# The last block of a four-block kernel: VectorE in the order written, Mamba steps spread singly

## The chip, the cores and the metric

The kernel runs on one core of a Trainium2 chip. The metric is the device time of one execution in microseconds (us). A core has five engines that run side by side and meet through semaphores: TensorE (PE; its weight loads are shown apart as PEld), VectorE (DVE), ScalarE (ACT), GpSimd (POOL) and SyncE (SP), which issues DMAs here. Each engine takes its own instructions in the order in which they stand in its queue.

## The reference

The input is `x`, 4 sequences of 1024 tokens with 128 channels. Four blocks follow each other, each of the form

```
xn = layernorm(x)
s  = attention-like layer(xn)
g  = silu(ffn-like layer(xn))
x  = x + s * g
```

Blocks 0 to 2 have softmax attention for `s` (16 heads of 8) and a channel mix or experts for `g`. The change is in block 3. There `s` is a Mamba-2 layer:

```
h       = layernorm(xn) * ln_w + ln_b
z, xBC, dt = split(h @ in_proj)
dt      = softplus(dt + dt_bias)
xBC     = silu(causal convolution of 4 taps over time (xBC))
state_t = state_(t-1) * exp(dt_t * A) + (dt_t * x_t) B_t;   y_t = state_t C_t + D * x_t
y       = y * silu(z);  y = y * rsqrt(mean(y^2) + eps) * rms_w
s       = xn + y @ out_proj
```

with 4 heads of 64 and 64 states. `g` is silu of a two-layer transformer on `xn` with 8 heads of 64, a local attention (windows of 64 tokens that look at themselves and the window before), and a gated GELU feed-forward of width 341. The two layers do not depend on each other until `s * g`.

## The kernel before

The kernel is written in a framework with tiles. The program is traced in the order in which Python emits instructions ("the order written"); then a planner orders each engine's instructions by its own estimate of when they can run. An instruction that is given to `keep_in_program_order` keeps its place on its engine. In the whole kernel all matmuls and transposes are kept so. For VectorE there is a wrapper, class `_Kept` (line 49): while its flag `on` is set, each VectorE instruction emitted through it is kept in the order written as well. The attention loops of blocks 0 to 2 set the flag (lines 561 to 591); before block 3 the plain `nc` is put back (`k.nc = nc`), so the planner orders VectorE there. ScalarE and GpSimd are ordered by the planner throughout.

Block 3 (`_block3`) weaves three lists of steps together; a step is a Python closure that emits some instructions:

- `local` (843 steps, the first 11 of them a lead-in): the two-layer transformer, 2 x 4 x 8 = 64 tiles of 128 tokens. In each turn of the loop over tiles, in this order: `scores` of tile i (TensorE into `lsc`, then VectorE's maxima `top` and `nb`), `turn` of i-1 (transposes `pt_ps`, copies `pT` on VectorE and ScalarE), `query` of i+2 (`qk_ps`; VectorE's rotation `qn`, `rot`; ScalarE's squares `sq`), `turn_out` of i-2, `key` of i+2, `weights` of i (8 exponentials `pr` on ScalarE), `to_fm` of i+1 (`qkt_ps`), `mix` of i-1 (`lo_ps`, then `rec` and `on`), `norms` of i+2 (VectorE's `ss`, GpSimd's power `rn`, line 1573, and scalings `qn`, `r8`), `out` of i-2 and `values` of i+2. Up to three places a tile, called `beside`, take a step from a side list: the shift of the next sequence, and for every four tiles the feed-forward `glu` as `[norm, None, normed, None, to_fm, gates, hidden, close]`, in the second layer followed by two steps that finish the output (`xn` on GpSimd, then the add into `x_end` on VectorE) with a `None` between. A `None` takes a place and emits nothing.
- `slots` from `_mamba` (206 slots, each a list of steps): the Mamba layer in 8 halves of 512 tokens. `put(at, step)` places a half's steps in slots around `at = 3 + 25 * h`: layer norm, transposes, projections of three channel groups (`project`, TensorE `xp_ps`, ScalarE into `cb`), the raw time steps, softplus, convolutions (`conv`, four VectorE instructions each into `xc`), running sums, gates (`z_ps`, then silu of `z` and `xc` on ScalarE), and then four chunks of 128 tokens, each with six steps from `exponents` (`xt_ps`, `r_ps`, `dec`) over `weights`, `products` (`y_ps`) and `turn` (`yt_ps`) to `norm` and `out` (`mo_ps`).
- `late`: what is left of block 2 (57 steps), at the block's start.

A layer norm has two halves: `_layernorm_parts` (line 80) computes mean and variance on VectorE (`ln_st`, `ln_mv`, `ln_ve`) and the factor `ln_rs` by a power on GpSimd (line 91), and returns a closure, called `normed` by its users, that scales the data on VectorE (line 95, four instructions). The small tiles of it have two buffers. All PSUM tiles of block 3 share a ring of eight buffers, so a matmul waits until the tile eight allocations back has been read.

`_interleave` emits from its lists in proportion to their lengths: first `local[:11]` with the first 9 slots, then the rest of `local` with the other 197 slots, where each slot's steps are emitted together. What is left of the feed-forward at the end (9 steps) follows.

Of the kernel before, what the change touches and what calls it, by code (L numbers as in the profile page):

```python
# [25 lines left out]
ALU = mybir.AluOpType  # L26
# [161 lines left out]
def _run(steps):  # L188
    for step in steps:
        if step:  # L190
            step()
# [960 lines left out]
def _mamba(k, t, wp, pool):  # L1152
# [6 lines left out]
    nc = k.nc  # L1159
    s = k.s  # L1160
    NH, HP, NS = 4, 64, 64
    ZX, HT = 644, 512
# [13 lines left out]
    conv_w = w3[:, ZX : ZX + 12].rearrange("p (g j) -> p g j", j=4)  # L1176
    conv_b = w3[:, ZX + 12 : ZX + 15]
# [10 lines left out]
    carry = wp.tile([P, 3, 3], F32, name="carry3")  # L1188
    dim = [P, 4, NH]

    def half_steps(h):
        v = Ctx()
        hf, n0 = h % 2, 4 * h
# [20 lines left out]
            matmul(xp, lhsT=w_in[:, c0 : c0 + P], rhs=v.xm, start=True, stop=True)  # L1214
            nc.scalar.copy(cb[:, 3 : HT + 3], xp)

        def conv(gq):
            if gq == 2:
                v.xc = pool.tile([P, 3, HT], F32, name="xc", bufs=1)
            cb = v.cb.pop(gq)  # L1220
            if hf == 0:
                nc.gpsimd.tensor_copy(carry[:, gq, :], cb[:, HT : HT + 3])
            acc = v.xc[:, gq, :]
            nc.vector.tensor_scalar(acc, cb[:, 0:HT], conv_w[:, gq, 0:1], conv_b[:, gq : gq + 1], ALU.mult, ALU.add)
            for j in range(1, 4):
                nc.vector.scalar_tensor_tensor(
                    acc, cb[:, j : j + HT], conv_w[:, gq, j : j + 1], acc, ALU.mult, ALU.add
                )
# [10 lines left out]
        def softplus():  # L1239


            raw, e = v.raw, v.e
            z, z2 = (pool.tile(dim, F32, name=f"dt_{i}", bufs=1) for i in "za")
            nc.vector.tensor_scalar_add(z, e, 2.0)
            nc.vector.reciprocal(z, z)
            nc.vector.tensor_tensor(z, z, e, ALU.mult)
            nc.vector.tensor_tensor(z2, z, z, ALU.mult)
            nc.vector.tensor_scalar_mul(e, z2, 2.0 / 17)
            for d in (15, 13, 11, 9, 7, 5, 3):
                nc.vector.scalar_tensor_tensor(e, e, 2.0 / d, z2, ALU.add, ALU.mult)  # L1250
            nc.vector.scalar_tensor_tensor(e, e, 2.0, z, ALU.add, ALU.mult)
            v.dt = pool.tile(dim, F32, name="dt", bufs=2)
            nc.vector.scalar_tensor_tensor(v.dt, raw, 0.0, e, ALU.max, ALU.add)
            v.da = pool.tile(dim, F32, name="da", bufs=2)
            nc.vector.tensor_tensor(v.da, v.dt, ea.unsqueeze(1).to_broadcast(dim), ALU.mult)
# [38 lines left out]

        v.cb = {}
        v.norm, v.to_fm, v.project, v.conv, v.raw_dt = norm, to_fm, project, conv, raw_dt
        v.softplus, v.sums, v.gates, v.weigh = softplus, sums, gates, weigh
        return v

    def chunk_steps(v, h, c, before):  # L1300
# [100 lines left out]
    slots = {}  # L1401

    def put(at, *steps):
        slots.setdefault(at, []).extend(steps)

    before = None
    for h in range(2 * B):
        v = half_steps(h)
        at = 3 + 25 * h
        put(at - 3, v.norm)  # L1410
        put(at - 2, lambda v=v: v.normed())
        put(at - 1, v.to_fm)
        put(at, v.raw_dt, lambda v=v: v.project(2))
        put(at + 1, v.softplus)
        put(at + 2, lambda v=v: v.conv(2), lambda v=v: v.project(0))
        put(at + 3, lambda v=v: v.conv(0), lambda v=v: v.project(1))
        put(at + 4, v.sums)
        put(at + 5, lambda v=v: v.conv(1))
        put(at + 6, v.gates)
        put(at + 7, v.weigh)  # L1420
        for c in range(4):
            u = before = chunk_steps(v, h, c, before)
            first = at + 8 + 4 * c
            for i, step in ((0, u.exponents), (1, u.weights), (3, u.products), (5, u.turn), (6, u.norm), (7, u.out)):
                put(first + i, step)
# [507 lines left out]
def _block3(k, t, out):  # L1933

    nc = k.nc
    s, xn = k.s, k.xn
    outv = out.rearrange("b (n p) c -> p (b n) c", p=P)
    with k.tc.tile_pool(name="w4", bufs=1) as wp, k.tc.tile_pool(name="l3", bufs=1) as pool, k.tc.tile_pool(
        name="ps3", bufs=1, space=PSUM
    ) as k.ps:  # L1940
        NW = 512 + 2 * HID + 384 + 8
        r4 = wp.tile([P, 2, 256], F32, name="r4")
        nc.sync.dma_start(r4.rearrange("p l c -> p (l c)"), t["r4"].to_broadcast([P, 512]))
        w4 = wp.tile([P, 2, NW], F32, name="w4")
        wqkv1 = wp.tile([P, 1536], F32, name="wqkv1")
        ends = {}

        def fetch(n):
            ends[n] = pool.tile([P, 4, C], F32, name="x_end", bufs=1)
            nc.sync.dma_start(ends[n], k.parked[n // 2][:, 4 * (n % 2) : 4 * (n % 2) + 4, :])  # L1950

        def finish(n, part):
            a = slice(4 * n, 4 * n + 4)
            if part == 0:
                nc.scalar.activation(xn[:, a, :], xn[:, a, :], AF.Silu)
                k.dump(3, n, s[:, a, :], xn[:, a, :])
                nc.gpsimd.tensor_tensor(xn[:, a, :], s[:, a, :], xn[:, a, :], ALU.mult)
            else:
                x = ends.pop(n)
                nc.vector.tensor_tensor(x, x, xn[:, a, :], ALU.add)  # L1960
                nc.sync.dma_start(outv[:, a, :], x)


        NW2 = 14 * P
        nc.sync.dma_start(w4[:, 1, 0:1024], t["w2"][:, 6 * P : NW2])
        nc.sync.dma_start(w4[:, 1, 1024:1030], t["w2"][:, NW2 + 6 : NW2 + 12])
        nc.sync.dma_start(w4[:, 1, 1030:1158], t["r2"][:, 2 * P : 3 * P].to_broadcast([P, P]))
        first, late = _late_steps(k, pool, w4[:, 1])
        _run(first)
        slots = _mamba(k, t, wp, pool)  # L1970
        local, begin, last = _local_layers(k, pool, w4, (k.wqkv0, wqkv1), r4, t["xpos"], xn, fetch, finish)
        _local_consts(k, pool)
        nc.sync.dma_start(w4[:, 0], t["w4"][:, 0, 1536:])
        late.append(lambda: nc.sync.dma_start(w4[:, 1], t["w4"][:, 1, 1536:]))
        nc.sync.dma_start(wqkv1, t["w4"][:, 1, 0:1536])

        def run(slot):
            for step in slot:
                step()


        slots = [lambda slot=slot: run(slot) for slot in slots]
        early = len(late) // 3
        _interleave(local[:begin], slots[:9], late[:early])

        n = 8 * (len(local) - begin) // (2 * NTILE + 2)
        m = n * (len(slots) - 9) // (len(local) - begin)
        _interleave(local[begin : begin + n], slots[9 : 9 + m], late[early:])
        _interleave(local[begin + n :], slots[9 + m :])
        run(last)  # L1990
# [3 lines left out]
def tile_blocks(ctx: ExitStack, tc: tile.TileContext, t, out, dump=None):  # L1994
    nc = tc.nc
    k = Ctx()
# [56 lines left out]
    k.parked = [tc.dram_tile([P, NT, C], F32, name=f"x{b}") for b in range(B)]  # L2053
    k.nc = _Kept(nc, tc)
    _blocks012(k, t)
    k.nc = nc
    stream.close()
    with tc.tile_pool(name="early3", bufs=1, side="right") as wp:
        _weights3(k, t, wp)
# [131 lines left out]
```

## Time and profile before

| | |
|---|---|
| time, median of 3 runs | 3529.68 us (3518.91 to 3532.71) |
| profiled execution, time | 3530.33 us |
| profiled execution, span from first to last instruction | 3528.6 us |
| granted TensorE clock, mean of the span | 0.960 |
| TensorE busy | 3137.5 us, 89% |
| VectorE busy | 2458.7 us, 70% |
| ScalarE busy | 1985.6 us, 56% |
| GpSimd busy | 1415.6 us, 40% |
| last block (2430 to 3530 us): TensorE, VectorE, ScalarE, GpSimd busy | 986.6, 829.3, 673.5, 691.0 of 1100 us |
| last block: granted clock | 0.93 |

A group row of the profile gives line, engine, operation, out<-in, shapes and count, then busy time and mean duration in ns, then the engine's idle time just before and what ended it. "A <- B: t, n, m" in a table of waits says that A stood idle for B, t us in n waits, the longest m. The granted clock is the share of TensorE's full clock that was given in a stretch. TensorE's ends are modelled, so its busy time is a reading of how densely it was fed.

### The profile page before, as it was taken

The numbers are of one execution on the slowest core, as the hardware profiler recorded it, in microseconds if no ns is written. First come the engines' busy times: TensorE is split into PE (matmuls) and PEld (weight loads), VectorE is DVE, ScalarE is ACT, GpSimd is POOL, SyncE is SP. The second block draws the span as 40 slices with busy tenths as digits, with TensorE's granted clock in tenths as the row PEclk, the third lists the DMA queues.
The fourth block names the chain that finished last, engine by engine and source line by source line (L and its number), as shares of the span: only waits on it lengthen the run. The fifth ranks groups of instructions, "written<-read, shape, count | busy, mean of one in ns | idle before, by whom it ended". The sixth has DMA issues, their size and how long they took to land.

```text
span 3528.6 us, 63440 instructions
## 1 busy us (share of the span) xinstructions
PE 3137.5 (89%) x23982; PEld 1693.8 (48%) x24121; DVE 2458.7 (70%) x4929; ACT 1985.6 (56%) x4191; POOL 1415.6 (40%) x1969
## 2 busy tenths in 40 slices
PE   4898988999989988889998989986899989989997
PEld 3444445664434434422333323322666767766665
DVE  7667663447777865788785686844788778777675
ACT  2444453346555554455666766664665656666664
POOL 5555553003323251120340321014766656755653
PEclk8999999999999999999999999998899999999999
DMA  3322312201222211011111211102110011011010
GB/s 101 71 63 55 73 42 87 59 28 47 52 50 60 42 51 31 21 45 28 39 45 45 66 35 26 30 7 73 29 37 16 20 25 24 18 24 28 21 27 21
DMA packets 134085, 146.61 MB, mean 42 GB/s; under 512 B 80642, under 2 KB 108298, under 8 KB 126474
## 3 DMA queue, kind: packets, MB, share of 16 engines
q1 hardware_dynamic: 131732, 138.34, 16.3%
q0 software_dynamic: 2048, 4.20, 0.4%
q8 instruction: 191, 3.13, 0.4%
q14 instruction: 114, 0.93, 0.1%
HBM read 94.42 MB, written 30.11 MB: 35 GB/s over the span
## 4 chain that ended last, share of the span: by engine, by line
PE 58%; DVE 19%; ACT 9%; POOL 8%; issue 4%; DMA 2%; SPq 0%; ACTq 0%; POOLq 0%; DVEq 0%
PE o_ps L104 11%; PE max_ps L104 10%; PE sc L104 10%; DVE neg L60 6%; ACT pt L451 4%; PE op L104 4%; PE hp L104 3%; POOL rn L1573 2%; PE proj_ps L104 2%; PE lsc L1481 1%; PE lo_ps L1481 1%; PE ag_ps L1481 1%; PE qk_ps L1481 1%; PE wo_ps L1481 1%; DVE xn L60 1%
## 5 line engine op out<-in xcount | busy, mean ns | idle before, releaser
L451 ACT ACTIVATE pt<-sc 128x512 f32<-128x512 f32 (+3 forms) x2432 | 1076.2, 512 | 754.1 <-PE sc L104 698.1
L60 DVE TENSOR_REDUCE neg<-max_ps 128x1 f32<-128x1024 f32 (+6 forms) x1088 | 1171.9, 1101 | 443.6 <-PE max_ps L104 404.8
L104 PE MATMUL sc<-q,k 128*128 128x512 bf16 (+3 forms) x2399 | 643.1, 340 | 94.6 <-ACT pt L451 69.0
L104 PE MATMUL max_ps<-k,q 128*128 128x512 bf16 (+3 forms) x2200 | 611.2, 347 | 73.8 <-DVE neg L60 50.7
L104 PE MATMUL o_ps<-pt,va 128*32 128x512 f32 (+3 forms) x4864 | 562.6, 526 | 16.8 <-POOL pt L421 9.1
L421 POOL TENSOR_SCALAR_AFFINE_SELECT pt<-pt 128x256 f32<-128x256 f32 (+2 forms) x768 | 291.3, 397 | 541.7 <-ACT pt L451 537.0
L104 PEld LDWEIGHTS <-k 128*128 128x128 bf16 x2432 | 185.6, 98 | 531.5 <-issue 415.9
L104 PEld LDWEIGHTS <-q 128*128 128x128 bf16 x2304 | 217.1, 99 | 357.6 <-issue 245.6
L1643 ACT ACTIVATE pr<-lsc,nb,r 128x128 f32<-128x128 f32 x512 | 201.2, 476 | 67.9 <-DVE nb L1635 67.7
L1564 POOL TENSOR_TENSOR qn<-qn,rot 128x512 f32<-128x512 f32 x128 | 166.1, 1303 | 157.8 <-DVE rot L1556 133.2
L1573 POOL TENSOR_TENSOR rn<-ss,neghalf 128x16 f32<-128x16 f32 x64 | 188.5, 2945 | 60.5 <-DVE ss L1571 48.3
L104 PEld LDWEIGHTS o_ps<-pt,va 128*32 128x32 f32 x4864 | 100.1, 109 | 227.1 <-issue 170.8
L196 POOL CAST negp<-neg 128x32 bf16<-128x32 f32 x48 | 10.1, 211 | 477.2 <-DVE neg L60 477.1
L91 POOL TENSOR_TENSOR ln_rs<-ln_ve,neghalf 128x4 f32<-128x4 f32 x72 | 73.8, 1026 | 262.0 <-DVE ln_ve L60 246.5
L728 ACT ACTIVATE h<-hp,eb 128x512 f32<-128x512 f32 x128 | 80.8, 683 | 163.2 <-PE hp L104 157.2
L1481 PE MATMUL qk_ps<-wqkv,hT 128*128 128x512 f32 x256 | 139.2, 628 | 23.7 <-DMA wqkv<-in_w_dram 7.3
L104 PE MATMUL hp<-xT,ew 128*128 128x512 f32 x256 | 127.9, 624 | 15.5 <-DVE neg L60 12.5
L60 DVE SCALAR_TENSOR_TENSOR xn<-op,gates,xn 128x128 f32<-128x128 f32 x256 | 72.0, 344 | 99.2 <-PE op L104 99.2
L104 PEld LDWEIGHTS op<-ew,h 128*128 128x128 f32 x1024 | 124.3, 194 | 19.6 <-issue 16.3
L104 PE MATMUL max_ps<-mask_window,ident 128*128 128x268 bf16 (+1 forms) x432 | 127.0, 294 | 0.0
L104 PE MATMUL op<-ew,h 128*128 128x128 f32 x1024 | 126.2, 277 | 0.1
L104 PEld LDWEIGHTS <-ident 128*128 128x128 bf16 x864 | 85.2, 99 | 65.5 <-issue 24.6
(368 smaller groups left out, 5483.9 us busy)
## 6 DMA issues: line engine op xcount, KB each, us to landing
q<-qx SPq DMA_DIRECT2D x144, 192.0 KB
k<-kx SPq DMA_DIRECT2D x432, 64.0 KB
va<-vb SPq DMA_DIRECT2D x120, 128.0 KB
qx<-qp SPq DMA_DIRECT2D x12, 768.0 KB
kx<-kp SPq DMA_DIRECT2D x12, 768.0 KB
ew<-in_e1w_dram SPq DMA_DIRECT2D x64, 128.0 KB
x<-x SPq DMA_DIRECT2D x16, 512.0 KB
x<-in_x_dram SPq DMA_DIRECT2D x8, 512.0 KB
```

The source lines that it names most:

```text
L60: r = op(*args, **kw)
L91: nc.gpsimd.tensor_tensor(rs, ve, k.neghalf[:, :n], ALU.pow)
L104: k.tc.keep_in_program_order(k.nc.tensor.matmul(*args, **kw))
L196: eng.tensor_copy(dst[:, 0], src)
L421: nc.gpsimd.affine_select(out=pt, in_=pt, pattern=[[0, 2], [step, pt.shape[2]]], compare_op=ALU.is_ge, fill=0.0, base=base, channel_multip ...
L451: nc.scalar.activation(pt[:, j % 2, :width], sc[:, :width], AF.Exp, scale=scale)
L728: nc.scalar.activation(h[:, hh, :], hp[:, hh, :], AF.Gelu, bias=eb1[:, e, hh : hh + 1])
L1481: pin(nc.tensor.matmul(*args, **kw))
L1564: nc.gpsimd.tensor_tensor(qn[:, i], qn[:, i], rot, ALU.add)
L1573: nc.gpsimd.tensor_tensor(rn, ss.rearrange("p w h -> p (w h)"), k.neghalf[:, : 2 * NH], ALU.pow)
L1643: nc.scalar.activation(t.pr[:, h, :], t.sc[r][:, c, :], AF.Exp, bias=t.nb[r][:, c : c + 1], scale=t.r8[:, h : h + 1])
```

## The change

Four things change, all in block 3:

1. The wrapper stays in use (`k.nc = nc` goes), and `_block3` sets its flag before it weaves the lists, so VectorE's instructions stand in the order written. (They then carry the wrapper's line, L60, in a profile.)
2. From slot 9 on, the Mamba slots are no longer emitted as units: their steps are put in one list, one entry each, an empty slot giving one empty entry (329 entries in place of 197 slots).
3. A convolution is split into two steps of two instructions each, with the next group's projection between the two for groups 2 and 0; the softplus is split into two steps (`softplus`, `series`), both in the same slot.
4. The Mamba layer norm's first half moves from slot `at - 3` to `at - 7`, its second half from `at - 2` to `at - 5` (not below slots 0 and 1).

```diff
-        def conv(gq):
-            if gq == 2:
+        def conv(gq, part):
+            if gq == 2 and part == 0:
                 v.xc = pool.tile([P, 3, HT], F32, name="xc", bufs=1)
-            cb = v.cb.pop(gq)
-            if hf == 0:
-                nc.gpsimd.tensor_copy(carry[:, gq, :], cb[:, HT : HT + 3])
+            cb = v.cb[gq] if part == 0 else v.cb.pop(gq)
             acc = v.xc[:, gq, :]
-            nc.vector.tensor_scalar(acc, cb[:, 0:HT], conv_w[:, gq, 0:1], conv_b[:, gq : gq + 1], ALU.mult, ALU.add)
-            for j in range(1, 4):
+            if part == 0:
+                if hf == 0:
+                    nc.gpsimd.tensor_copy(carry[:, gq, :], cb[:, HT : HT + 3])
+                nc.vector.tensor_scalar(
+                    acc, cb[:, 0:HT], conv_w[:, gq, 0:1], conv_b[:, gq : gq + 1], ALU.mult, ALU.add
+                )
+            for j in (1,) if part == 0 else (2, 3):
                 nc.vector.scalar_tensor_tensor(
                     acc, cb[:, j : j + HT], conv_w[:, gq, j : j + 1], acc, ALU.mult, ALU.add
                 )
...
             nc.vector.tensor_scalar_mul(e, z2, 2.0 / 17)
+            v.z, v.z2 = z, z2
+
+        def series():
+            raw, e, z, z2 = v.raw, v.e, v.z, v.z2
             for d in (15, 13, 11, 9, 7, 5, 3):
...
         at = 3 + 25 * h
-        put(at - 3, v.norm)
-        put(at - 2, lambda v=v: v.normed())
+        put(max(at - 7, 0), v.norm)
+        put(max(at - 5, 1), lambda v=v: v.normed())
         put(at - 1, v.to_fm)
         put(at, v.raw_dt, lambda v=v: v.project(2))
-        put(at + 1, v.softplus)
-        put(at + 2, lambda v=v: v.conv(2), lambda v=v: v.project(0))
-        put(at + 3, lambda v=v: v.conv(0), lambda v=v: v.project(1))
+        put(at + 1, v.softplus, v.series)
+        put(at + 2, lambda v=v: v.conv(2, 0), lambda v=v: v.project(0), lambda v=v: v.conv(2, 1))
+        put(at + 3, lambda v=v: v.conv(0, 0), lambda v=v: v.project(1), lambda v=v: v.conv(0, 1))
         put(at + 4, v.sums)
-        put(at + 5, lambda v=v: v.conv(1))
+        put(at + 5, lambda v=v: v.conv(1, 0), lambda v=v: v.conv(1, 1))
...
-        slots = [lambda slot=slot: run(slot) for slot in slots]
+        slots = [lambda slot=slot: run(slot) for slot in slots[:9]] + [
+            step for slot in slots[9:] for step in slot or [None]
+        ]
+        k.nc.on = True
         early = len(late) // 3
...
     _blocks012(k, t)
-    k.nc = nc
     stream.close()
```

More of the change, by code (lines that the diff above doesn't have):

```diff
@@ L1296, in half_steps @@
         v.norm, v.to_fm, v.project, v.conv, v.raw_dt = norm, to_fm, project, conv, raw_dt
-        v.softplus, v.sums, v.gates, v.weigh = softplus, sums, gates, weigh
+        v.softplus, v.series, v.sums, v.gates, v.weigh = softplus, series, sums, gates, weigh
         return v
```

## The prediction

> **What bounds the kernel now.** The change touches only the last block, so I first read the table of stretches for it: its start, its steady part (the 64 attention tiles) and its tail. The columns are the stretch, its length, the busy time and instruction count of each engine, the granted TensorE clock, the DMA share and GB/s.
>
> ```profile
> 2430.00:2530.00 100.00, 68.18 (x565) 45.67 (x566) 72.82 (x207) 49.23 (x95) 76.82 (x94) 0.80 0.20 57
> 2530.00:3477.00 947.00, 884.79 (x9566) 637.49 (x9568) 736.57 (x2074) 607.08 (x1285) 607.89 (x602) 0.94 0.11 24
> 3477.00:3530.00 53.00, 33.59 (x280) 22.87 (x278) 19.90 (x59) 17.18 (x29) 6.28 (x8) 0.86 0.05 16
> ```
>
> TensorE bounds it: in 947 us it is idle for 62.2 us only, and the next engine, VectorE (DVE), is busy for 737. But the clock is 0.94, so up to 0.06 x 947 = 57 us more of full-speed work is lost. What makes TensorE idle? It waits for VectorE, and VectorE waits for GpSimd (POOL). The waits of VectorE in the last block (who waits for whom, us in total, times, longest):
>
> ```profile
> DVE top L1632 <- PE lsc L1481: 39.2, 26, 2.9
> DVE sh L95 <- POOL ln_rs L91: 38.6, 13, 7.8
> DVE x_end L1960 <- POOL xn L1957: 19.2, 5, 5.3
> ...
> DVE ln_x L95 <- POOL ln_rs L91: 14.0, 3, 5.8
> DVE ss L1385 <- ACT sq L1382: 14.0, 9, 4.4
> ```
>
> The first row is harmless: VectorE has caught up with TensorE. The next three are a norm's second half, or the closing add, standing on VectorE before GpSimd has its factor. One such place in the chain that ended last (start, us, what):
>
> ```profile
> 2765.68 1.16 DVE ss L1571
> ...
> 2766.91 2.94 POOL rn L1573
> ...
> 2769.91 1.04 POOL qn L1574
> ...
> 2771.36 1.05 POOL ln_rs L91
> ...
> 2772.43 1.11 DVE sh L95 x4
> 2773.54 1.20 DVE top L1632 x2
> ...
> 2774.81 0.61 DVE pT L1653
> ...
> 2775.47 2.17 PE qkt_ps L1484 x8
> ```
>
> The norm's factor `ln_rs` queues on GpSimd behind `rn` (2.94), `qn` (1.04) and `r`: 5.3 us with its own 1.05. VectorE has `sh` next and sits idle for 3.95 us, though `top`, behind it, had its scores at 2767.7 (the matmuls end at 2766.45 + 1.21). So `top`, the exponentials and `pT` are late, TensorE finds no free PSUM buffer and stops for 3.05 us. What that costs shows in the stretches before, in, and after the stop:
>
> ```profile
> 2755.00:2771.00 16.00, 16.00 (x206) 12.31 (x195) 12.17 (x35) 10.36 (x22) 11.03 (x11) 1.00 0.18 35
> 2771.00:2775.00 4.00, 1.41 (x6) 0.58 (x6) 2.57 (x8) 0.10 (x1) 1.27 (x2) 0.95 0.01 2
> 2775.00:2785.00 10.00, 9.53 (x62) 8.22 (x63) 7.34 (x22) 6.58 (x17) 6.21 (x7) 0.51 0.01 2
> ```
>
> For 10 us after the stop the clock is halved: two `qk_ps` matmuls take 2.07 us in such a place and 1.02 elsewhere. Ten stops of this kind stand in the steady part of the timeline (VectorE's wait, then TensorE's idle time): 3.95 and 3.05 at 2772; 4.65, 3.82; 4.76, 3.44; 4.08, 2.52; 3.95, 3.38; 2.69, 1.83; 5.77, 3.90; 3.85, 1.58; 4.39, 3.40; 5.25, 3.86 at 3391. TensorE's sum is 30.8 us, half of its idle 62.2.
>
> **VectorE in the order written.** It adds and removes no instruction (4931 on VectorE both ways). Before, the planner of the framework put `sh` directly behind its sums. As written, an empty step stands between a norm's sums and its second half, about half a tile to one tile (8 to 16 us) later, and one between the two parts of the closing; in the order the new program has on VectorE, both scores of the next tile, `pT` and two projections stand between. That exceeds the 5.3 us GpSimd needs, so nine stops go (the tenth, `ss` behind `sq`, gets about 7 us from turn to norm and goes too). Idle time saved: 30.8 us.
>
> *The clock.* The Trainium skill, page "TensorE: Matmul & The Clock Gate", section "HAM oscillation", says that only idle gaps over about 3.4 us cost the clock. By it four of the ten stops pay (3.82, 3.44, 3.90, 3.86). The trace has half clock after eight of the ten, from 1.58 us (plus another 1.2 close by) and 3.05 us up, for 68.2 us, with TensorE busy 9.3 + 12.0 + 6.5 + 3.4 + 6.8 + 6.4 + 5.3 + 9.8 = 59.4 us. At full clock that work takes half: 29.7 us saved, by the rule's four stops (35.0 busy) 17.5. The measured eight decide; I take 25, since short matmuls follow the clock less.
>
> *The start.* `cl_ps` waits 10.39 us for `da`, as the 15 small instructions of the softplus (0.16 to 0.19 us each) were laid between convolutions and rotations from 2458.5 to 2469.8. As written they follow each other: 15 x 0.17 = 2.6, at the row's mean of 0.256 3.8 us. Saved: about 7.5; taken 8 with a little clock.
>
> *What else could it cost?* In a fixed order anything not ready blocks all behind it. By the times of before, most producers are done when TensorE passes the instruction's place in the new order. Exceptions: `wdt` (last of ScalarE's row after the gates; 8 places, at most 2.3 us late) and `dt_z` (8, at most 4.1). Behind them stand rotations and `ss`; TensorE has the ring of eight PSUM buffers before it notices. Bounds 0 and 8 x 6.4 = 51 us; the ten stops show that about 0.8 us of a wait is absorbed and most of these places have slack, so I take 5.
>
> **Slots step by step.** 197 slots become 329 single steps over the same 832 attention steps: one per 2.5 attention steps instead of a slot (one to four steps) per 4.2, so at 13.2 attention steps per 15.9 us tile 3.0 us against 5.1. All engines' work stays. The Mamba chain's distances on TensorE change; I laid the new TensorE order on the times of before:
> - products to turn (32): median 10.2 us before, 6.4 after, smallest 2.3. The chain between (`y`, `yi` on VectorE, `y` twice on GpSimd) ends 4.0 to 10.8 us after the first product, median 6.1; the products themselves give 2.3 more. At the median the shortfalls sum to 4.4 us, at 7.5 us to 16. Taken 5.
> - gates to first exponents (8): 10.7 before, 4.0 after. The last `xc` leaves ScalarE at -4.0 to +4.2 us from the gates' start, TensorE needs it at 4.1 to 8.1. Bounds 0 and 8 x 3; taken 4.
> - exponents to products in a half's first chunk (8): 5.3 to 17 us, needing 6.9 minus 1.2; taken 2, at the longest chain (12.8) 19.
> Their sum, 11, and the 5 above are 16 us lost, with ends 0 and about 110.
>
> **Convolutions in two steps.** Four instructions of 0.64 + 3 x 0.80 = 3.0 us become 1.4 and 1.6. It issues no more. The `cb` ring has two buffers: `project(1)` must await the second part of `conv(2)`, now one step (3 us) ahead; GpSimd's copy and ScalarE's eviction stand behind. Such waits for `xc` cost GpSimd 12.5 us in 840 now, idle time off the path. Taken 0, bounds -5 and +10.
>
> **Norm four slots sooner.** Eight sums (0.27, 0.165), an add, four scalings (about 0.5) on VectorE and one power (1.04) on GpSimd per half, no DMA. The sums and the second half now stand two to three steps, 6 us or more, apart. TensorE's own waits for `ln_x` (2.0 us in all) go: -2. It passes only the previous half's last chunks on VectorE and GpSimd; its 5 us are hidden by VectorE's 20% of idle time.
>
> **Sum.** -30.8 - 25 - 8 - 2 + 16 = -50 us. The profiled execution took 3530.3 us (span 3528.6), so 3480; the median of runs is 3529.7, which leaves 3480.
> A second way: six tiles, from 2615.2 to 2703.4, ran without a stop at clock 1.00 in 88.2 us, 14.7 each; all 63 tile periods average 15.9. If all ran at 14.7, 75 us would go. The sum stays inside this.
>
> **Rivals.**
> 1. *Quiet pace everywhere*: the stops with other causes go too. 75 + 8 from 3530 gives 3447. For it: VectorE was 80% busy in the quiet stretch (70.3 of 88.2). Against: seven stops of the steady part have table loads or `qn` as last releaser.
> 2. *Hidden*: the Mamba chain's shorter distances and VectorE's head waits return what the stops gave: 16 becomes 60, giving about 3525. For it: 48 places have less distance. Against: in the median they still fit.
> 3. *Slower*: GpSimd's `y` becomes the wait at turn. GpSimd holds `rn` for 2.94 us a tile; if half of the 32 turns wait 3 us and each brings 6.8 us of half clock (0.44 lost per us), 16 x 6.0 = 96 us come back: 3530 - 66 + 96 = 3560. It decides from 66 / 32 = 2.1 us per turn. Against: the median turn has 8.7 us for 6.1.
> 4. *The change does nothing*: excluded, as the built order on VectorE differs throughout the block.
>
> **How the numbers follow.** Chances: my sum 0.60 (its own range 3450 to 3510), rival 1 0.17, rival 2 0.12, rival 3 0.11. A measurement of this kernel can tell about 0.5%, 17.6 us: faster 0.77, same 0.12, slower 0.11. The range 3430 to 3535 reaches to rival 1 below, with some of what lies beyond the quiet pace, and takes in rival 2.
>
> **What would show it.** Right: VectorE's waits for `ln_rs` and for `xn` at the closing nearly vanish, the clock of the steady part rises from 0.94 to 0.97 or more, its TensorE idle time falls from 62 to below 45, and `cl_ps` waits 3 us. Wrong: TensorE's or its weight loads' waits at `yt_ps`, `xt_ps` or `y_ps` sum to over 40 us, or VectorE waits for `wdt`, `dt_z` or `ss` instead, at the same clock.

## The result, and the profile after

The changed kernel takes 3546.56 us (median of 11 runs, 3537.41 to 3552.26), the kernel before 3532.14 us in the runs beside it: a ratio of 1.0042, 95% interval 1.0032 to 1.0052. It is 0.4% slower; 1.4% faster was predicted (3480 from 3529.7), and 3546.56 lies outside the range of 3430 to 3535. The profiled execution took 3545.3 us with a span of 3543.3.

The table of stretches of the changed kernel (length, then TensorE, weight loads, VectorE, ScalarE, GpSimd busy, clock, DMA share, GB/s):

```profile
2430.00:2530.00 100.00, 71.07 (x568) 45.22 (x565) 76.22 (x207) 42.21 (x87) 76.11 (x95) 0.80 0.19 54
2530.00:3477.00 947.00, 868.14 (x9454) 617.26 (x9456) 786.44 (x2046) 605.81 (x1272) 599.23 (x591) 0.96 0.10 24
3477.00:3545.00 68.00, 48.26 (x394) 34.99 (x383) 29.02 (x82) 23.94 (x47) 16.19 (x19) 0.82 0.07 22
```

In the same 947 us the granted clock rose from 0.94 to 0.96, as the prediction wanted, but TensorE is idle for 78.9 us instead of 62.2, and got through 112 matmuls fewer. VectorE is busy 50 us longer (786.4 against 736.6), with no instruction more.

VectorE's waits in the last block of the changed kernel:

```profile
DVE top L60 <- PE lsc L1488: 33.3, 23, 6.4
DVE s L60 <- POOL rs L1394: 29.3, 14, 4.4
...
DVE ln_x L60 <- POOL ln_rs L91: 8.6, 1, 8.6
```

The row `sh <- ln_rs` (38.6 us in 13 waits) has shrunk to one wait of 1.1 us. A new row stands there: `s`, the last step of a Mamba chunk, waits 29.3 us for its factor `rs` from GpSimd. TensorE's waits from 2530 us on:

```profile
PE yt_ps L1170 <- POOL y L1378: 15.8, 8, 4.8
PE y_ps L1167 <- POOL xdt L1342: 9.8, 5, 3.0
PE qkt_ps L1491 <- POOL qn L1581: 8.0, 7, 3.6
PE ag_ps L1488 <- DVE gT L60: 6.3, 4, 4.0
```

Before, the largest were these, and neither of the two Mamba rows was among the first:

```profile
PE qkt_ps L1484 <- DVE pT L1653: 10.7, 4, 3.9
PE ag_ps L1481 <- DVE gT L1720: 6.0, 2, 5.1
```

Now the three largest are waits for GpSimd. One such place in the chain that ended last (start, us, what):

```profile
2970.57 1.27 POOL qn L1571
2971.84 0.53 POOL rs L1394
2972.39 0.35 DVE s L60
...
2972.87 0.42 DVE on L60
...
2973.84 1.20 DVE ss L60 x2
...
2975.32 2.91 POOL rn L1580
...
2978.30 1.04 POOL qn L1581
...
2979.73 0.73 POOL y L1367
...
2980.53 0.73 POOL y L1378
```

and its end on TensorE's timeline (start, us, what, idle time before it and who ended that):

```profile
2975.47 1.02 PE L1488 MATMUL qk_ps<-wqkv,hT 128*128 128x512 f32 x2
2981.31 0.69 PE L1170 MATMUL yt_ps<-ident,y 128*128 128x128 f32 x2 [4.82 <-POOL y L1378]
```

`rs` stands on GpSimd behind a rotation's addition. VectorE has `s` next and stops for 1.84 us; behind it, in the written order, stand `rec`, `on` and then `ss`, the norm of a later tile. So `ss` ends late, and GpSimd, which has `rn` next, is idle for 2.96 us. VectorE's own parts of `y`, whose products TensorE finished at 2971.6, come after `ss`, at 2975.3 to 2976.1. GpSimd's parts then stand behind `rn`, `qn` and `r` and begin at 2979.7, and the turn on TensorE waits for them. So a wait of 1.84 us at the head of VectorE's queue has gone through GpSimd's queue into another layer's chain. It can account for 1.84 of TensorE's 4.82 us at most. The rest comes from the order itself: VectorE's parts of `y` stand behind `ss`, and so GpSimd's parts stand behind `rn`, `qn` and `r`, which take 4.2 us.

### The profile page after: what moved, and what is told of

The parts are those of the page before. It is cut to its first block, busy times and chain, and to the rows that moved or that the text cites. A ratio compares the mean times of both kernels' runs of the same rounds, so it can differ in the third digit from the quotient of the medians.

```text
span 3543.3 us, 63508 instructions
## 1 busy us (share of the span) xinstructions
PE 3138.7 (89%) x23984; PEld 1686.5 (48%) x24121; DVE 2523.1 (71%) x4929; ACT 1985.1 (56%) x4188; POOL 1418.3 (40%) x1969
## 4 chain that ended last, share of the span: by engine, by line
PE 54%; DVE 21%; POOL 10%; ACT 8%; issue 4%; DMA 2%; SPq 0%; POOLq 0%; ACTq 0%; DVEq 0%
PE o_ps L104 11%; PE max_ps L104 10%; PE sc L104 9%; DVE neg L60 6%; ACT pt L451 4%; PE op L104 4%; PE hp L104 3%; POOL rn L1580 2%; PE ag_ps L1488 2%; PE proj_ps L104 2%; DVE xc L60 2%; DVE xn L60 1%; DVE ss L60 1%; PE lo_ps L1488 1%; PE lsc L1488 1%
## 5 line engine op out<-in xcount | busy, mean ns | idle before, releaser
L60 DVE TENSOR_REDUCE neg<-max_ps 128x1 f32<-128x1024 f32 (+6 forms) x1088 | 1172.8, 1103 | 442.8 <-PE max_ps L104 413.4
L104 PE MATMUL o_ps<-pt,va 128*32 128x512 f32 (+3 forms) x4864 | 560.8, 524 | 16.9 <-POOL pt L421 9.1
L60 DVE SCALAR_TENSOR_TENSOR xn<-op,gates,xn 128x128 f32<-128x128 f32 x256 | 72.1, 345 | 99.2 <-PE op L104 98.8
```

The costliest lines, as they stand in the source:

```text
L60: r = op(*args, **kw)
L104: k.tc.keep_in_program_order(k.nc.tensor.matmul(*args, **kw))
```

## The experiments

Every ratio is to the kernel before, from runs on the same chip, with its 95% interval. The table collects what I read from each trace: tiles (of 64) whose transposes on TensorE begin less than 0.4 us after GpSimd's last scaling of `qn`; turns (of 32) that begin less than 0.4 us after `y`; products (of 32) likewise after `dec` and `xdt`; and the time at half clock from 2530 us on, in the one profiled execution. A short link has next to no slack, and TensorE often stood waiting there: in the changed kernel it waited over 0.15 us 7 times for `qn` and 8 times for `y`. One execution says little of the clock (e3's profiled one, at 0.961, is below the median of e3's runs), so the column "clock" gives the mean granted clock in the median of all of a kernel's runs, and in brackets that of the kernel before beside it.

| kernel | VectorE | slots | short: `qn` | short: turn | short: products | half clock, us | clock | ratio |
|---|---|---|---|---|---|---|---|---|
| before | planner | whole | 2 | 0 | 0 | 119 | 0.960 to 0.962 | 1 |
| changed | written | single | 17 | 11 | 8 | 91 | 0.965 | 1.0042 |
| e1_order_alone | written | whole | 13 | 1 | 0 | 55 | 0.967 (0.962) | 0.9977 |
| e2_steps_alone | planner | single | 4 | 2 | 7 | 106 | 0.964 (0.962) | 0.9996 |
| e3_slots_whole | written | whole | 12 | 2 | 0 | 103 | 0.965 (0.962) | 0.9956 |
| e5_planner_order | planner | single | 4 | 5 | 4 | 98 | 0.964 (0.962) | 1.0017 |
| e6_norms_first | written | single | 7 | 13 | 7 | 82 | 0.968 (0.962) | 1.0049 |
| e7_turn_later | written | single | 20 | 0 | 7 | 99 | 0.964 (0.962) | 1.0010 |
| e8_whole_norms_first | written | whole | 6 | 2 | 0 | 62 | 0.967 (0.962) | 0.9944 |
| e9_half_power | written | single | 6 | 12 | 7 | 61 | 0.969 (0.962) | 0.9978 |
| e10_room | written | single | 19 | 0 | 5 | 115 | 0.962 (0.960) | 1.0093 |
| e11_before_half_power | planner | whole | 2 | 0 | 0 | 58 | 0.968 (0.960) | 0.9876 |
| e12_gates_later | written | whole | 8 | 2 | 0 | 47 | 0.970 (0.960) | 0.9915 |
| e13_norms_turn | written | single | 3 | 0 | 10 | 56 | 0.970 (0.961) | 0.9986 |
| e14_room_norms | written | single | 11 | 0 | 6 | 86 | 0.966 (0.961) | 1.0049 |
| e15_split_power | written | whole | 7 | 2 | 0 | 52 | 0.969 (0.961) | 0.9941 |

### The parts one by one

**e1_order_alone**: the kernel before, with VectorE's order fixed and nothing else.

```diff
+        k.nc.on = True
...
-    k.nc = nc
```

> The kernel before with VectorE kept in the order written in the last block, nothing else changed. Theory A (the written order takes the ten stops away as predicted, and the shorter Mamba distances of the single steps give it back, GpSimd's part of the chain being late at turn and products): this keeps the old distances, so it is faster than before by 30 to 60 us (ratio 0.983 to 0.992), with TensorE's waits at yt_ps and y_ps no longer than before (about 15 us together). Theory B (the fixed order on VectorE is itself the loss, since what is not ready blocks what stands behind): about +15 us or more, ratio 1.003 to 1.010, with VectorE waiting for GpSimd's rs or for ScalarE.

3519.42 us against 3526.26: 0.9977 (0.9965 to 0.9989). The order helps, by 7 us, where the prediction's terms for it (30.8 + 25 + 8 less 5) come to 59. Its profiled execution (3512.1 us, one of its faster ones) shows what it saves and what takes its place. VectorE's waits for `ln_rs` ahead of `sh` are down to one of 1.1 us, and half clock falls from 119 to 55 us; by the runs' clock, 0.967 against 0.962, the typical gain is about half of that. But TensorE's stops of over 0.3 us from 2530 us on sum to no less: 72.5 us, 67.5 before. Those over 1.5 us fell from 55.3 us (19 stops) to 46.7 (17); shorter ones rose from 12.2 us (20) to 25.8 (33). The largest of them on VectorE's timeline:

```profile
2608.75 0.53 DVE L60 TENSOR_SCALAR xc<-cb,w 128x512 f32<-128x512 f32 x1
2609.32 2.33 DVE L60 SCALAR_TENSOR_TENSOR xc<-cb,w,xc 128x512 f32<-128x512 f32 x3
2611.56 0.68 DVE L60 TENSOR_TENSOR qn<-qk_ps,tab 128x512 f32<-128x512 f32 x1
2612.16 0.74 DVE L60 TENSOR_TENSOR rot<-qk_ps,tab 128x256 f32<-128x256 f32 x2
2612.83 2.09 DVE L60 TENSOR_SCALAR xn<-x_end,ln_mv,ln_rs 128x128 f32<-128x128 f32 x4
2614.84 0.80 DVE L60 TENSOR_SCALAR gT<-tr_ps,w 128x512 f32<-128x512 f32 x1
```

and on TensorE's, with the same place in the kernel before under it:

```profile
2615.69 2.07 PE L1481 MATMUL ag_ps<-gT,w 128*128 128x512 f32 x2 [6.30 <-DVE gT L60]
```

```profile
2607.31 4.54 PE L1481 MATMUL ag_ps<-gT,w 128*128 128x512 f32 x6 [5.13 <-DVE gT L1720]
```

VectorE never stops here. Its order puts a convolution, a rotation and the scaling of `xn`, 6.1 us together, directly ahead of `gT`, whose transposes had ended at 2604.8, and the gates are TensorE's next matmul: it stops for 6.30 us. This stop is not new: the planner, too, had put convolution, rotation and `xn` ahead of `gT`, so it only grew by 1.2 us. What is new is the number of such places. Over the whole block waits for `gT` are 11.5 us in 4 waits (6.0 in 2 before), those for `qn` 14.7 in 7 (3.8 in 2 before), those for `ln_x` 15.8 in 8 (2.0 in 4 before). A second sign of lateness: a tile's `ss` begins 3.4 us after its squares in the median, 1.0 before. The written order has `rec` and `on` of another tile ahead of it; with the norms first (e8) it is 1.9 us.

The order also makes VectorE's own work longer, which the prediction left out. A norm's sums as written, in e1, and in the planner's order, in the kernel before:

```profile
2603.95 0.29 DVE L60 BATCH_NORM_STATS2 ln_st<-x_end 128x6 f32<-128x128 f32 x1
2604.27 0.18 DVE L60 BATCH_NORM_AGGREGATE ln_mv<-ln_st 128x2 f32<-128x6 f32 x1
2604.37 0.26 DVE L60 BATCH_NORM_STATS2 ln_st<-x_end 128x6 f32<-128x128 f32 x1
```

```profile
2452.23 0.16 DVE L87 BATCH_NORM_AGGREGATE ln_mv<-ln_st 128x2 f32<-128x6 f32 x1
2452.31 0.26 DVE L86 BATCH_NORM_STATS2 ln_st<-x_end 128x6 f32<-128x128 f32 x1
2452.49 0.16 DVE L87 BATCH_NORM_AGGREGATE ln_mv<-ln_st 128x2 f32<-128x6 f32 x1
```

The planner separates an instruction from the one whose result it reads, and each starts some 0.08 us before the end of its neighbour. As written, the reader stands directly behind the writer and starts 0.03 us after its end. In the last block 746 VectorE instructions of e1 start just after the end of their neighbour (by less than 0.15 us), 140 before; 606 times 0.11 is some 67 us, an estimate. VectorE's busy time there is 880.5 us against 828.9; it is 828 to 830 in all versions of the planner's order and 880 to 906 in all of the written one. How much of TensorE's short stops comes from this was not tested by itself.

**e2_steps_alone**: the kernel before, with single steps from slot 9 on.

```diff
-        slots = [lambda slot=slot: run(slot) for slot in slots]
+        slots = [lambda slot=slot: run(slot) for slot in slots[:9]] + [
+            step for slot in slots[9:] for step in slot or [None]
+        ]
```

> The kernel before with the Mamba slots emitted as single steps, VectorE still ordered by the planner. Theory A: the stops behind ln_rs stay and the short distances come on top: slower than before by 20 to 60 us (ratio 1.006 to 1.017), with new TensorE waits at yt_ps and y_ps of 15 us or more. Theory B: the steps are neutral, ratio 0.998 to 1.003.

0.9996 (0.9986 to 1.0007): under the planner single steps cost nothing that can be measured.

**e3_slots_whole**: the changed kernel with whole slots (the diff above, undone).

> The changed kernel with its Mamba slots emitted as whole slots again (written order on VectorE, split convolutions and the sooner norm stay). Theory A: faster than before by 30 to 60 us (ratio 0.983 to 0.992), that is 45 to 75 us faster than the change, and the waits at yt_ps and y_ps fall back to about 15 us. Theory B: within 10 us of the changed kernel, ratio 1.002 to 1.007.

3511.67 us, 0.9956 (0.9941 to 0.9971). Beside e1 it has the split convolutions and the sooner norm, and TensorE's waits of 8.7 us for `ln_x` from 2530 us on are gone. Beside the changed kernel: single steps cost 1.0042 - 0.9956, that is 30 us, once VectorE's order is fixed.

**e5_planner_order**: the changed kernel with the planner's order on VectorE.

```diff
-        k.nc.on = True
```

> The changed kernel with VectorE ordered by the planner (single steps, split convolutions and the sooner norm stay). Theory A: the stops behind ln_rs return, so it is slower than the changed kernel by 20 to 60 us, ratio to before 1.009 to 1.020. Theory B: about the time of before, ratio 0.997 to 1.002.

1.0017 (1.0004 to 1.0030). So single steps cost nothing (e2) to 0.2% (e5) under the planner, the written order alone gains, and the pair costs 30 us. Two measures show where the pair differs. The planner keeps short `qn` links at 4 in both of its single-step versions; in the written order they are 12 or more, with single steps or without. And the chain from a chunk's first product to its finished `y` takes 5.2 and 5.4 us in the median with single steps under the planner (e2, e5) and 6.8 in the changed kernel, while with whole slots it is 6.1 before and 6.0 in e1.

### Two links, one at a time and together

**e6_norms_first**: the changed kernel, `ss` of tile i+2 ahead of `rec` and `on` of tile i-1.

```diff
-        at(i - 1, "mix")
         at(i + 2, "norms")
+        at(i - 1, "mix")
```

> The changed kernel with each tile's norms emitted ahead of the mix of the tile before, so that VectorE's sums ss no longer stand behind rec and on. Theory C (the fixed order makes ss late: in the changed kernel the second ss starts 3.5 us after its square is there, in the median, against 1.0 before, so GpSimd's power rn starts later in every tile, and that is where the attention's share of the expected gain went): the median falls to about 1 to 1.5 us, TensorE's waits at qkt_ps for qn (7.5 us) go, and the kernel is 15 to 30 us faster than the changed one (ratio to before 0.995 to 1.000). Theory D (the lost time lies in the Mamba chain's short distances alone): the same time as the changed kernel within 5 us, ratio 1.003 to 1.006, whatever ss does.

1.0049 (1.0030 to 1.0067), no gain. The short `qn` links fall from 17 to 7, but `yt_ps` still waits 14.0 us for `y`.

**e7_turn_later**: the changed kernel, `turn`, `norm` and `out` of each chunk one slot later.

```diff
-(5, u.turn), (6, u.norm), (7, u.out)
+(6, u.turn), (7, u.norm), (8, u.out)
```

> The changed kernel with turn, norm and out of each Mamba chunk one slot later, which puts the turn four steps behind the products instead of two: by the times of before a median of 14.3 us in place of 6.4 (10.2 in the kernel before). Theory D: TensorE's waits at yt_ps (15.6 us after 2530) fall below 5 us, and the kernel is 15 to 30 us faster than the changed one (ratio 0.995 to 1.000). Theory C: the waits at yt_ps fall too, but another wait takes their place, and the time stays within 8 us, ratio 1.002 to 1.006.

3531.15 us, 1.0010 (1.0000 to 1.0020), 11 us better than the change. No turn is short any more; 20 tiles are, at `qn`. The edit moves `norm` and `out` as well, and VectorE's waits of `s` for `rs`, 29.3 us in the changed kernel, are gone with those of the turn, so the 11 us cannot be put down to the turn alone.

**e8_whole_norms_first**: e3 with the norms first.

> The changed kernel with whole slots, 0.9956 of before as measured, and norms ahead of mix as well. Theory C: another 10 to 25 us off, ratio 0.988 to 0.993, with the half clock and the waits at qkt_ps for qn reduced. Theory D: no further gain, ratio 0.994 to 0.998.

0.9944 (0.9929 to 0.9959), 4 us better than e3, which their intervals do not separate.

**e10_room**: e7 with two empty steps after `weigh` and two more in a half's first chunk, to give the other Mamba links back their distance.

```diff
-        put(at + 7, v.weigh)
+        put(at + 7, v.weigh, lambda: None, lambda: None)
+        put(at + 10, *[lambda: None] * 3)
```

> The changed kernel with turn, norm and out of each chunk one slot later, two empty steps after `weigh` and two more between the first chunk's exponents and its products (32 more empty entries in the list of single steps). Theory D (the shortened distances of the Mamba chain are what single steps cost under the fixed order, 30 us between this list and the whole slots): the waits of `y_ps` for `xdt` (22 us in the changed kernel, engine and weight loads together) and of `yt_ps` for `y` (35 us) vanish, the number of chunks with less than 0.4 us of slack falls to 2 or fewer in both links, and the ratio to the kernel before is 0.995 to 0.998. Rival (it is the single steps' VectorE and GpSimd work, laid between attention work more finely, that disturbs the attention): the Mamba waits vanish and the ratio stays at 1.000 to 1.002, where the later turn alone was (1.001).

3563.19 us, 1.0093 (1.0071 to 1.0116), the slowest of all. The theory that distances in the Mamba chain alone explain the 30 us falls: TensorE waits 0.9 us at `yt_ps` and 0.9 at `y_ps`, and the kernel lost 29 us against e7. Its TensorE waits from 2530 us on:

```profile
PE qkt_ps L1492 <- POOL qn L1582: 18.2, 11, 3.9
PE dt_ps L1167 <- DVE xm L60: 9.6, 5, 2.8
PE tr_ps L1492 <- DVE sh L60: 9.5, 8, 4.0
```

All three are other chains' links: the tile's norm, the projection of the time steps, the feed-forward's transposes. The 32 empty entries also bring all the others closer together (832 attention steps over 361 entries are 2.3 for each, in place of 2.5); which of the two did the harm is open.

**e13_norms_turn**: the changed kernel with the edits of e6 and e7 together. **e14_room_norms**: e10 with the edit of e6.

> The changed kernel with both single remedies together: the norms of tile i+2 ahead of the mixing of tile i-1 (alone 1.0049), and turn, norm and out of a chunk one slot later (alone 1.001). Theory E (single steps under the fixed order make two links of the chain short at once, the norms' `qn` before its transposes, 17 of 64 tiles without slack, and the Mamba links, and each remedy left the other one short): tiles without slack before their transposes fall to 8 or fewer, no `yt_ps` wait for `y`, ratio 0.994 to 0.998, near the whole slots. Rival F (single steps spoil the fixed order in another way, as the list with more empty steps at 1.0093 suggests): the links get their slack and the ratio stays at 1.000 or above.

> The slowest version so far (later turn and 32 more empty entries in the list of single steps, 1.0093, where 19 of 64 tiles had no slack before their transposes and TensorE waited 18 us for `qn`), with the norms of a tile ahead of the mixing. Theory E: the waits for `qn` nearly vanish and the ratio falls by 0.008 or more, to 0.995 to 1.001. Rival F: it falls by less than 0.004, to 1.005 or above.

e13: 3522.99 us, 0.9986 (0.9976 to 0.9995). e14: 1.0049 (1.0033 to 1.0065). Each lies between the two theories, e14 nearer to the second. The norms-first edit, worth nothing that shows on the changed kernel, is worth 1.0010 - 0.9986 = 8 us where the turn has its distance, and 1.0093 - 1.0049 = 16 us on e10, where its 18.2 us of waits for `qn` leave only one of 2.9. So the norm's link is a real cost, but mending it paid only where the turn no longer stopped TensorE. Together the two edits return 20 of the 35 us between the changed kernel and e8. The other 15 us stay open. What e13 still shows:

```profile
PE dt_ps L1167 <- DVE xm L60: 6.4, 4, 2.2
...
PE y_ps L1167 <- POOL xdt L1342: 4.2, 4, 2.8
```

are two more links. The second, exponents to products, is one that single steps shorten (10 short products, none with whole slots). The first, `to_fm` to the time steps, waits as long with whole slots (6.3 us in 2 waits in e1). No run mended these alone.

### GpSimd's power, and the urgent instruction

**e9_half_power**: the changed kernel with the power `rn` on 8 of its 16 columns. **e11_before_half_power**: the same in the kernel before. Both leave out the queries' norm and use the keys' factor in its place, so they measure a cost and are no versions to keep.

```diff
-nc.gpsimd.tensor_tensor(rn, ss.rearrange("p w h -> p (w h)"), k.neghalf[:, : 2 * NH], ALU.pow)
+nc.gpsimd.tensor_tensor(rn[:, NH : 2 * NH], ss[:, 1], k.neghalf[:, :NH], ALU.pow)
...
-nc.gpsimd.tensor_scalar_mul(r8, rn[:, 0:NH], 8.0)
+nc.gpsimd.tensor_scalar_mul(r8, rn[:, NH : 2 * NH], 8.0)
```

> The changed kernel with GpSimd's power rn on 8 columns instead of 16 (the queries' norm is left out, the keys' stands in its place). It takes the row of 2.93 us to about 1.6, 64 times. If GpSimd's queue is what both the turn and qkt_ps wait for (theory C and D agree on it), the changed kernel gets 25 to 60 us faster, ratio 0.987 to 0.997. If the waits only moved to VectorE's fixed order, it gains less than 10 us, ratio above 1.001.

> The kernel before, with the power `rn` on 8 of its 16 columns: the queries' norm is left out and the keys' factor stands in its place. GpSimd's 2.94 us a tile become about 1.5. If the stops behind `ln_rs` and GpSimd's queue are as costly under the planner as the prediction took (66 us for the stops, in which `ln_rs` stands behind `rn` for 2.94 of 5.3 us), half of each stop goes: 15 us of idle time and some clock, ratio 0.992 to 0.996. If GpSimd's queue matters only where VectorE's order is fixed (the half power gained 23 us there): ratio 0.998 to 1.000.

e9: 3518.57 us, 0.9978 (0.9967 to 0.9989), 23 us less than the change. e11: 3486.04 us, 0.9876 (0.9855 to 0.9897), 44 us less than before, and more than expected. The group row of e11 on GpSimd, and its steady stretch:

```profile
L1573 POOL TENSOR_TENSOR rn<-ss,neghalf 128x8 f32<-128x8 f32 x64 | 107.6, 1682 | 59.4 <-DVE ss L1571 46.9 <-DVE ss L1385 7.3 <-DVE ln_mv L87 2.2
```

```profile
2530.00:3477.00 947.00, 890.77 (x9836) 640.46 (x9835) 754.51 (x2130) 623.65 (x1312) 541.00 (x609) 0.97 0.11 25
```

1.26 us a tile came off an engine that is busy 64% of the stretch. TensorE's stops of over 0.3 us fall from 67.5 to 48.9 us and half clock from 119 to 58 us; at half pace that is up to 30 us more, so 49 in all for the 44 measured. VectorE's wait for `ln_rs` ahead of `sh` is still there, 28.2 us instead of 38.6: only a quarter of it went, so the gain cannot be put down to the ten stops alone.

**e12_gates_later**: e8, with an empty step between the feed-forward's transposes and its gates.

```diff
-        return [norm, None, lambda: held.normed(), None, to_fm, gates, hidden, close]
+        return [norm, None, lambda: held.normed(), None, to_fm, None, gates, hidden, close]
```

> VectorE in the order written, whole slots, sooner norm, the norms of a tile first (the version at 0.9944), and an empty step between the feed-forward's transposes and its gates. If TensorE's waits for `gT` (4 or 5 waits, 11 to 13 us, in all versions with whole slots and fixed order) are an urgent instruction that stands behind other work in VectorE's fixed order, and are not paid elsewhere: the waits of `ag_ps` for `gT` fall below 4 us, and with half clock gone the ratio is 0.990 to 0.993. If VectorE's lateness there is simply that it has too much to do in this stretch, the stop moves to another wait and the ratio stays at 0.993 to 0.996.

3500.16 us, 0.9915 (0.9894 to 0.9935): the fastest complete version, 30 us less than before. The waits of `ag_ps` for `gT` fall from 12.7 us in 5 to

```profile
PE ag_ps L1488 <- DVE gT L60: 2.6, 2, 1.7
```

which is the expected sign. Its gain over e8, 10 us, is the size expected; the two intervals overlap a little.

**e15_split_power**: e12 with the power in two, the keys' half and their scaling ahead of the queries' half.

```diff
-            nc.gpsimd.tensor_tensor(rn, ss.rearrange("p w h -> p (w h)"), k.neghalf[:, : 2 * NH], ALU.pow)
+            nc.gpsimd.tensor_tensor(rn[:, NH : 2 * NH], ss[:, 1], k.neghalf[:, :NH], ALU.pow)
             nc.gpsimd.tensor_tensor(
                 qn[:, 1], qn[:, 1], rn[:, NH : 2 * NH].unsqueeze(2).to_broadcast([P, NH, D]), ALU.mult
             )
+            nc.gpsimd.tensor_tensor(rn[:, 0:NH], ss[:, 0], k.neghalf[:, :NH], ALU.pow)
```

> The best complete version so far (0.9915: whole slots, norms first, gates one step later) with the power in two: the keys' 8 columns, their scaling, and only then the queries' 8 columns. The keys' factor comes some 1.3 us sooner, GpSimd's work grows by the fixed part of one more instruction (some 0.2 to 0.3 us a tile). If half the power is worth so much because the keys' factor comes sooner: ratio 0.985 to 0.990. If because GpSimd's queue gets shorter for all else (`ln_rs`, `y`): ratio 0.990 to 0.995, not better than 0.9915.

0.9941 (0.9924 to 0.9957): no better than e12, rather 9 us worse. GpSimd's instruction times in the last block sum to 726 us, 702 in e12. So an earlier factor for the keys did not pay for a queue that is some 24 us longer. It may still be worth a little: at the rate of e11, 44 us for some 77 us less of GpSimd's time, the longer queue would by itself cost about 13 us, an estimate. Most of what e9 and e11 gained is thus put down to the time in GpSimd's queue; the two effects were not separated further.

## Why the prediction was wrong

Term by term, by the medians: the order alone was to bring -59 us (-30.8 - 25 - 8 + 5) and brought -7; single steps were to cost 11 and cost 30; the rest was to bring -2 and brought -8.

*The ten stops and the clock (-30.8 and -25)*: that these waits go was right. The `sh` waits fall from 38.6 us to between 1 and 3 in every version with the written order, and `x_end <- xn` goes from 19.2 us to 3.4. What they were worth in time is not shown by itself, since other stops came at once. The clock's term was too large: among the runs of the kernel before, 0.001 of mean clock goes with 1.9 to 2.7 us on the four chips used, so the 0.005 that the order alone gained is worth some 10 to 13 us, an estimate. That short matmuls follow the clock less is so: in the kernel before one of 128x512 takes 0.59 us at full clock and 1.06 at half, one of 64x64 0.22 and 0.31. The rule that the prediction cites, read as "only gaps over 3.4 us cost the clock", does not hold here: the changed kernel has 19 pieces of half clock from 2530 us on, and 5 stops of TensorE that are longer than 3.4 us.

*What else could it cost (5 us)*: this is the step that failed. It said that "by the times of before, most producers are done when TensorE passes the instruction's place in the new order". It laid the new order of one engine on the old times of the others, and took VectorE's own work as unchanged. But `ss` itself moved back by 2.5 us in the median, and `rn` waits for it at the head of GpSimd's queue. The row of before, and of the changed kernel (2530 to 3480 us):

```profile
POOL rn L1573 <- DVE ss L1571: 46.0, 31, 7.2
```

```profile
POOL rn L1580 <- DVE ss L60: 103.5, 51, 5.6
```

GpSimd's busy time stayed the same; what moved is when its results come. Short `qn` links rose from 2 to 17, and to 13 by the order alone. The waits that I had looked for, `wdt` and `dt_z`, came to no more than 0.7 us; `s <- rs`, 29.3 us (6.4 with the order alone), did come, and I had not listed it. Nor did I ask the opposite question, who waits for an instruction that now stands late behind others that are ready: `gT`, `ss`, `xm`, `ln_x`. In e1 TensorE's stops over 0.3 us would have been 36.7 us without the ten; they are 72.5. New and longer stops took the place of all that had gone.

*Slots step by step (11 us)*: mis-sized, and treated as if it added to the order's part. Measured: 0 to 5 us under the planner, 30 us under the written order. In the changed kernel TensorE's stops over 0.3 us ahead of Mamba matmuls are 32.9 us, 16.9 before, while those ahead of attention stay at 51.2 against 50.6. The new distance was forecast well: from the first product to the turn 6.4 + 2.3 = 8.7 us, and 9.2 measured (11.4 before). The chain that has to fit into it was not. I took 6.1 us from the median of before; after the change it takes 6.8, and 11 of 32 turns are short. It is the pair that lengthens it: single steps under the planner have 5.2 to 5.4.

*The start (-8)*: `cl_ps`'s wait fell from 10.4 us to under 1, as foreseen, and `x_ps` now waits 7.0 us once, because VectorE stands 8.6 us at its first `ln_x` with the rest of the start behind it. TensorE is busy 71.1 of the first 100 us instead of 68.2: 3 us are left of the 8.

*Convolutions (0) and the sooner norm (-2)*: together they are what separates e3 from e1, some 8 us, which the intervals do not quite separate; the norm is the likelier part, since the `ln_x` waits go. The order of GpSimd's and VectorE's instructions side by side brought one thing that I had not counted:

```profile
L60 DVE SCALAR_TENSOR_TENSOR xc<-cb,w,xc 128x512 f32<-128x512 f32 x72 | 70.4, 978 | 1.9
```

The same 72 instructions took 801 ns each before (875 with the order alone); 12.8 us of VectorE's time went here. The traces show where. In the kernel before, the first of these two lies inside a power `rn` of GpSimd, and the second beside two rotations' additions:

```profile
2461.30 0.75 DVE L1226 SCALAR_TENSOR_TENSOR xc<-cb,w,xc 128x512 f32<-128x512 f32 x1
2465.23 1.81 DVE L1226 SCALAR_TENSOR_TENSOR xc<-cb,w,xc 128x512 f32<-128x512 f32 x1
```

```profile
2459.11 2.90 POOL L1573 TENSOR_TENSOR rn<-ss,neghalf 128x16 f32<-128x16 f32 x1
2464.01 2.48 POOL L1564 TENSOR_TENSOR qn<-qn,rot 128x512 f32<-128x512 f32 x2
```

Of the 72 in the changed kernel, 33 overlap a GpSimd addition or scaling of `qn` and take 1.25 us in the mean; the other 39, of which 13 lie wholly inside a power, take 0.75. Before, 14 of the 72 overlapped one.

*The account of the whole*: stops over 0.3 us cost 16.6 us more (84.1 against 67.5). All of it is in stops of 0.3 to 1.5 us: 40 of them with 29.9 us, 20 with 12.2 before, while the longer ones are 54.2 and 55.3 us. The time TensorE was busy at half clock fell from 102.1 to 80.7 us, worth 10.7 us. The profiled execution is 15.0 us longer. So some 9 us are in the pace between: matmuls follow each other at larger distances without a stop that the rows show. I have no finer account of it.

*Rivals*: the third, "GpSimd's `y` becomes the wait at turn", has a right mechanism (15.8 us of waits and the chain shown above), but at 0.5 us per turn, far below the 2.1 from which it was to decide. The second, *hidden*, is the nearest in kind: the shorter distances and VectorE's head waits returned what the stops gave. It stopped at 60 us returned and should have gone to about 80 (a sum of -50 with 16 in it became +14). The signs named beforehand read mixed: waits for `ln_rs` gone and `cl_ps` short (right), idle time up instead of down (wrong), clock 0.96 where 0.97 was asked. One sign of being wrong came true: the waits of TensorE's weight loads at `yt_ps`, `xt_ps` and `y_ps` sum to 55.1 us from 2530 us on (34.6 before), over the 40 that were named.

## What to carry to other kernels

When one engine's order is fixed, list three things: what each instruction at the head of the queue may wait for, what urgent instruction now stands behind ready work, and where a reader now stands directly behind its writer. Carry the delays through the next engine's queue before using old times as margins. Two changes that are each harmless can be bad together when one takes away the slack that the other needs, so price them as a pair, and mend all links at once: mending the norm's link alone showed nothing here, and behind the turn's it gave 8 us. A shorter power on an engine that is idle for a third of the time was worth 44 us, the best reordering 30 (their intervals overlap slightly). So look at what stands in such a queue behind its longest instruction.

## What was not expected of the hardware

- GpSimd's power takes 2.93 us for 16 columns and 1.66 for 8, so 0.16 us a column; halving it was worth 44 us of 3530 although GpSimd is busy 64% of the stretch.
- A convolution instruction on VectorE takes 0.75 us alone or inside a GpSimd power, and 1.25 us in the mean where it overlaps GpSimd's addition or scaling of `qn` (128x512). `state * etot` goes the same way: 0.41 us, and 1.19 beside those (11 and 13 instructions of the changed kernel).
- A VectorE instruction that reads the result of the one directly before it starts 0.03 us after that one's end; one that reads something else starts 0.08 us before it. In e1 some 600 more such pairs go with 52 us more of busy time for the same instructions.
- Half clock came after stops well below 3.4 us, as after one of 2.23 us at 3307.9: 19 pieces in the changed kernel, with 5 stops over that length.
- Not of the hardware, but as little expected: empty steps, which emit nothing, moved the time by 29 us for 32 of them (e10 against e7). How two woven lists fall on each other is a quantity to be measured.
